# First sums of a graph network: three 14-column tiles for the gathered rows, indices and gathers a block ahead, the overflow added first, the byte stores one block late

## Chip, cores and metric

The kernel runs on one core of one Trainium2 chip. The metric is the device time of one execution in microseconds (us); the time before is the median of three runs. Profiles are of one execution.

## What is computed

The reference is a stack of four graph networks over 6,250 nodes (48 features) and 200,000 edges `src -> dst`. The change touches the first sum of the first network only. Cut to that:

```python
gate = silu(edge_attr @ F1W + F1b) @ F2W + F2b            # per edge
gate = gate + (ei * (ej @ adapt)).sum(-1, keepdims=True)  # ei, ej: embeddings of src and dst
cw   = where(distances < CUT, 0.5 * (cos(pi * distances / CUT) + 1.0), 0.0)
mj   = node_mult[dst]
msg  = gate * h[dst] * (cw * mj)[:, None]
agg  = segment_sum(msg, src, num_segments=N)
tot  = segment_sum(mj, src, num_segments=N)
```

All later layers use the same edges: four layers of attention over `src`, two convolutions, a gated sum, a normalised convolution. So this first pass also leaves in DRAM what they read.

## The kernel before

**Data.** The nodes stand in 49 blocks of 128 (one node per partition). An earlier stage, `build_grid`, has put one 138-number record per edge into DRAM. `grid` has one record per (tail node, head block): for a tail block these are 49 columns of 128 records. A second edge between a tail and the same head block goes to the overflow: `WS[b]` more columns for block `b`, 4 to 28, 502 in all, 10.25 on average.

**The loop.** `first_sums` walks over the 49 tail blocks in the list `ORDER`, whose neighbours have unlike numbers of overflow columns (4, 5, 14, 8, 12, 9, 11, 10, 7, 5, 28, 6 ...). For each block:

- The records come in tiles `recs` of at most 14 columns: four for the grid (14, 14, 14, 7; `load`, L1062, on SP's queue) and one for the overflow, two where it has over 14 columns (L1058).
- `heads_to_rows` copies the head numbers to `hd` (L1128), transposes them on TensorE (L1130), stores them in DRAM as `heads` (L1133) and reads them back, broadcast to all partitions, as `hr` (L1121).
- `hr` against the lane number gives one-hot tiles `hot_b` (L1187, DVE). ACT makes 8-bit copies and stores them for later layers (L1191, L1192).
- TensorE transposes each one-hot square; ACT gathers these in the tile `dt` (L1199, one buffer), a block's 128 rows of the adjacency matrix.
- TensorE picks the head rows of the table by matmuls with the one-hot squares (`pick_rows`, L1007); ACT copies them to `tr` (L1008, two buffers).
- `add` (L1152 to L1178) makes the messages of one piece of up to 14 columns and adds them to `acc`: nine to ten DVE instructions. L1160 adds to the bias, L1177 sums the weights to `ac`, L1165 to L1176 share the single tile `pr`. Two ACT copies with stores keep attributes and gates for later layers (L1155 to L1159).
- `put_rows` (L1231) stores `dt` into `adj` by an indirect DMA from POOL's queue.

**The overflow** can't be picked by one-hots. `overflow` (L1066 to L1108) reads its records, gathers `ei`, the tail's own row (L1073), makes the indices `idx_g` on DVE (L1082) and gathers each column's table rows into `tr_o` with one indirect DMA per column from POOL's queue (L1085). Then it counts how often a cell of `adj` occurs (`same`, `times`, L1090 to L1094) and makes the cell numbers `to` and the 8-bit counts `many` (the tile is named `times_8`, ACT, L1107). `put_cells` writes one byte per partition and column into `adj` (L1112, indirect DMAs on POOL's queue); these must come after the rows of the same block have been written.

**Order.** In the program's text a block does: one-hots; four pieces with their adds, and after the second the load of the next block's grid records; `heads_to_rows` of the next block; the adds of the overflow; the `adj` store; the final sums; `overflow` of the next block; the byte stores of this block. The framework that builds the program places instructions in each engine's queue by priority and by when it believes their operands to be ready, so a queue's order can differ from the text; `keep_in_program_order` (L1162) forbids this for one instruction. Each queue is worked in order. Tiles have a fixed number of buffers (`bufs`, else two in this pool), and an instruction that needs a new one waits for the last reader of the oldest.

Of the kernel before, what the change touches and what calls it, by code (L numbers as in the profile page):

```python
# [18 lines left out]
F32 = mybir.dt.float32  # L19
# [10 lines left out]
N, E, H, R, G, NEL, L = 6250, 200000, 48, 40, 32, 119, 4  # L30
P = 128
# [4 lines left out]
def rows(t, i):  # L36
    return bass.IndirectOffsetOnAxis(ap=t[:, i : i + 1], axis=0)
# [436 lines left out]
NB = 49  # L474
# [55 lines left out]
def chunks(n, k):  # L530
    return [(i, min(k, n - i)) for i in range(0, n, k)]
# [480 lines left out]
def first_sums(ctx: ExitStack, tc: tile.TileContext, g, keep, dram, table0, tails, h, agg, tot):  # L1012
# [39 lines left out]
    def load(b, spans, src):  # L1052

        out = []
        for s0, n in spans:
            t = sp.tile([P, PC, RW], F32, name="recs", bufs=8)
            if src is over:
                nc.sync.dma_start(t[:, :n], over[b, :, s0 : s0 + n])  # L1058
            else:
                for k in range(s0, s0 + n, GD):  # L1060
                    v = g.grid[k * NQ : (k + GD) * NQ].rearrange("(r d) f -> r d f", d=GD)
                    nc.sync.dma_start(t[:, k - s0 : k - s0 + GD], v[b * P : (b + 1) * P])  # L1062
            out.append(t)
        return out

    def overflow(b, hd):  # L1066


        W = WS[b]
        spans = chunks(W, PC)  # L1070
        recs = load(b, spans, over)
        ei = sp.tile([P, 2 * G + H], F32, name="ei")
        nc.gpsimd.indirect_dma_start(out=ei, out_offset=None, in_=tails, in_offset=rows(g.nat, b))  # L1073
        hv = hd[:, NB : NB + W]
        for (s0, n), t in zip(spans, recs):
            nc.vector.tensor_copy(hv[:, s0 : s0 + n], t[:, :n, HD])
        none = sp.tile([P, OS], F32, name="none", bufs=1)
        nc.vector.tensor_scalar(none[:, :W], hv, 0.0, None, OP.is_equal)
        nc.vector.tensor_scalar(g.bias[:, g.col[b] + NB : g.col[b] + NB + W], none[:, :W], -BIG, None, OP.mult)
        ix = g.idx[:, WO[b] : WO[b + 1]]  # L1080
        nc.vector.tensor_scalar(none[:, :W], none[:, :W], float(NQ), -1.0, OP.mult, OP.add)
        nc.vector.tensor_tensor(ix, hv, none[:, :W], OP.add)  # L1082
        tr = sp.tile([P, OS, T0], F32, name="tr_o", bufs=1)
        for w in range(W):
            nc.gpsimd.indirect_dma_start(out=tr[:, w], out_offset=None, in_=table0, in_offset=rows(g.idx, WO[b] + w))  # L1085

        mf = sp.tile([P, OS], F32, name="times", bufs=1)
        for w, n in chunks(W, 12):
            eq = sp.tile([P, 12, NB + OS], BF, name="same", bufs=1)
            nc.vector.tensor_tensor(eq[:, :n, : NB + W], hd[:, None, : NB + W].to_broadcast([P, n, NB + W]),  # L1090
                                    hv[:, w : w + n, None].to_broadcast([P, n, NB + W]), OP.is_equal)
            nc.vector.tensor_tensor(eq[:, :n, NB : NB + W], eq[:, :n, NB : NB + W],
                                    weights[:, w : w + n, :W], OP.mult)
            nc.vector.reduce_sum(mf[:, w : w + n], eq[:, :n, : NB + W], AX.X)  # L1094

        to = sp.tile([P, OS], I32, name="to")
        nc.vector.scalar_tensor_tensor(none[:, :W], mf[:, :W], float(AGAIN), none[:, :W], OP.is_ge, OP.add)
        nc.vector.tensor_scalar(none[:, :W], none[:, :W], -1.0, float(1 << 19), OP.not_equal, OP.mult)
        nc.vector.tensor_tensor(none[:, :W], none[:, :W], nat49[:, b : b + 1].to_broadcast([P, W]), OP.add)
        pl = sp.tile([P, OS], I32, name="pl", bufs=1)  # L1100
        nc.vector.tensor_scalar(pl[:, :W], ix, 7, None, OP.logical_shift_right)
        nc.vector.tensor_tensor(to[:, :W], pl[:, :W], none[:, :W], OP.add)
        nc.vector.tensor_scalar(to[:, :W], to[:, :W], 7, None, OP.logical_shift_left)
        nc.vector.tensor_scalar(pl[:, :W], ix, P - 1, None, OP.bitwise_and)
        nc.vector.tensor_tensor(to[:, :W], to[:, :W], pl[:, :W], OP.bitwise_or)
        many = sp.tile([P, OS // 4], I32, name="times_8")
        nc.scalar.activation(many.bitcast(F8)[:, :W], mf[:, :W], AF.Copy, saturate=False)  # L1107
        return [(NB + s0, n, rec, tr[:, s0 : s0 + n]) for (s0, n), rec in zip(spans, recs)], ei, (to, many)  # L1108

    def put_cells(b, to, many):  # L1110
        for w in range(WS[b]):
# [7 lines left out]
    def heads_of(b, d0, n):  # L1119
        hr = sp.tile([P, PC * P], BF, name="hr")  # L1120
        nc.sync.dma_start(hr[:, : n * P], heads[b : b + 1, d0 * P : (d0 + n) * P].to_broadcast([P, n * P]))  # L1121
        return hr

    def heads_to_rows(b, recs):

        hd = sp.tile([P, NB + OS], F32, name="hd")
        for (s0, n), t in zip(spans, recs):
            nc.vector.tensor_copy(hd[:, s0 : s0 + n], t[:, :n, HD])  # L1128
        pt = tp.tile([NB, P], F32, name="hd_ps")
        nc.tensor.transpose(pt, hd[:, :NB], ident)  # L1130
        ht = sp.tile([NB, P], BF, name="ht")
        nc.vector.tensor_scalar(ht, pt, firsts, None, OP.subtract)
        nc.sync.dma_start(heads[b].rearrange("(d p) -> d p", p=P), ht)  # L1133
        bs = g.bias[:, g.col[b] : g.col[b] + NB]
        nc.vector.tensor_scalar(bs, hd[:, :NB], 1.0, -1.0, OP.min, OP.add)
        nc.vector.tensor_scalar(bs, bs, BIG, None, OP.mult)
        return [heads_of(b, *span) for span in spans[:2]], hd

    recs = load(ORDER[0], spans, g.grid)
    hrs, hd = heads_to_rows(ORDER[0], recs)  # L1140
    others, ei, own_cells = overflow(ORDER[0], hd)
    for pos, b in enumerate(ORDER):
        after = ORDER[pos + 1] if pos + 1 < NB else None
        T = NB + WS[b]
        nc.scalar.copy(h[:, pos], ei[:, 2 * G :])
        lgt = sp.tile([P, NB + OS], F32, name="lgt")
        bs = g.bias[:, g.col[b] : g.col[b] + T]
        ac = sp.tile([P, 8, 1], F32, name="ac")
# [3 lines left out]
        def add(t0, n, rec, tr):  # L1152
            rec = rec[:, :n]
            at = sp.tile([P, PC, R], F32, name="at", bufs=2)
            nc.scalar.copy(at[:, :n], rec[:, :, :R])  # L1155
            nc.scalar.dma_start(g.attr[b, :, t0 : t0 + n], at[:, :n])
            g2 = sp.tile([P, PC, H], F32, name="g2", bufs=2)
            nc.scalar.copy(g2[:, :n], rec[:, :, R + H : CW])
            nc.scalar.dma_start(g.gate[b, :, t0 : t0 + n], g2[:, :n])  # L1159
            i = nc.vector.tensor_add(bs[:, t0 : t0 + n], bs[:, t0 : t0 + n], tr[:, :n, T0 - 1])  # L1160
            if t0 >= NB:
                tc.keep_in_program_order(i)  # L1162

            pr = sp.tile([P, PC, 2 * G], F32, name="pr", bufs=1)
            nc.vector.tensor_mul(pr[:, :n], tr[:, :n, H : H + 2 * G], ei[:, None, : 2 * G].to_broadcast([P, n, 2 * G]))  # L1165
            lg = sp.tile([P, PC, 2], F32, name="lg")
            nc.vector.reduce_sum(lg[:, :n], pr[:, :n].rearrange("p t (k g) -> p t k g", k=2), AX.X)
            nc.vector.tensor_mul(lg[:, :n, 0], lg[:, :n, 0], rec[:, :, CW])
            nc.vector.tensor_mul(lgt[:, t0 : t0 + n], lg[:, :n, 1], rec[:, :, CW])

            ga = pr[:, :, :H]
            nc.vector.tensor_add(ga[:, :n], rec[:, :, R : R + H], lg[:, :n, 0:1].to_broadcast([P, n, H]))
            if not done:
                nc.vector.memset(acc, 0.0)
            nc.vector.tensor_mul(ga[:, :n], ga[:, :n], tr[:, :n, :H])
            nc.vector.tensor_add(acc[:, :n], acc[:, :n], ga[:, :n])  # L1176
            nc.vector.reduce_sum(ac[:, len(done)], tr[:, :n, T0 - 2], AX.X)  # L1177
            done.append(t0)  # L1178


        dt = sp.tile([P, NB, P], F8, name="dt", bufs=1)
# [11 lines left out]
        for i, (s0, n) in enumerate(spans):  # L1193
# [8 lines left out]
            add(s0, n, recs[i], tr)  # L1202
            if i == 1 and after is not None:
                ahead = load(after, spans, g.grid)
        if after is not None:
            hrs, hd = heads_to_rows(after, ahead)
        for piece in others:
            add(*piece)
        i = put_rows(tc, g.adj, g.nat, b, dt.rearrange("p d q -> p (d q)").bitcast(I32), "adj")
        tc.declare_no_dep(i.ins, group="cells", reason="the cells before are in rows of other nodes")  # L1210
        cells_of = b, *own_cells
        nc.scalar.dma_start(g.logit[b, :, :T], lgt[:, :T])
        add_up(nc, acc, PC, agg[:, pos])
        nc.vector.reduce_sum(tot[:, pos : pos + 1], ac[:, : len(done)].rearrange("p i o -> p o i"), AX.X)
        if after is not None:
            recs = ahead
            others, ei, own_cells = overflow(after, hd)
        put_cells(*cells_of)


def add_up(nc, t, n, to):
# [622 lines left out]
```

## Time and profile before

| | us |
|---|---|
| median of 3 runs (lowest, highest) | 12119.19 (12105.58, 12132.64) |
| the profiled execution, its own time | 12122.53 |
| its span, first to last instruction | 12120.7 |
| 3760 to 6160 of the span, which holds the first sums | 2400.00 |
| of these: DVE busy | 1429.62 |
| POOL busy | 1193.94 |
| ACT busy | 1153.64 |
| PE busy | 819.84 |

The share of the 16 DMA engines in that part is 0.68 on average, at 221 GB/s. Busy times are sums over instructions of one engine; register work and the issue of DMAs by SP and ACT are not in them. An indirect DMA's row on POOL is the making of its descriptors; when its data lands is seen only from who waits for it. In the views, "<- X" names what released an instruction that had been waiting.

### The profile page before, as it was taken

Reading aid. Unit: us, or ns where it says so; the run is one execution under the profiler, and the core shown is the slowest. Engines: PE = TensorE matmul, PEld = TensorE weight load, DVE = VectorE, ACT = ScalarE, POOL = GpSimd, SP = SyncE. Lnnn points to the kernel's source line nnn. Section 1 sums busy time; section 2 is a strip of 40 time slices with the busy share of each in tenths; the row PEclk is TensorE's granted clock in tenths of the full one; section 3 lists DMA queues with packets and bytes.
Section 4 is the critical chain, followed back from the end, with each engine's and each line's share of the span. In section 5 each row is a group of like instructions: output and inputs, shape, how many; then the busy total and the mean of one; then the engine's idle time right before and its main releaser. Section 6 shows DMA issues by size and latency. Waiting matters only on the chain. (4 is left out here: it accounts for less than half of the span.)

```text
span 12120.7 us, 180061 instructions
## 1 busy us (share of the span) xinstructions
PE 5280.4 (44%) x67611; PEld 4656.0 (38%) x67611; DVE 7874.7 (65%) x16470; ACT 3855.5 (32%) x9495; POOL 7176.8 (59%) x5713
## 2 busy tenths in 40 slices
PE   1166555555452333333334444443444444582226
PEld 1144443344342333333234443443444344482226
DVE  7756555555554655566569888887988888515443
ACT  0044434334333544544433223222322222111111
POOL 0257555555554455545548886886888688408880
PEclk9986666666666666666656666666766667796558
DMA  8845222222225766667634434443443444555445
GB/s 292 288 142 171 71 64 67 67 64 67 67 66 165 238 211 220 225 218 231 202 115 129 129 119 119 127 126 105 137 125 119 124 124 130 164 167 145 130 125 153
DMA packets 970521, 1742.53 MB, mean 144 GB/s; under 512 B 478058, under 2 KB 686158, under 8 KB 911909
## 3 DMA queue, kind: packets, MB, share of 16 engines
q1 hardware_dynamic: 645378, 1038.72, 27.2%
q0 software_dynamic: 188320, 315.39, 10.9%
q10 hardware_dynamic: 135936, 376.80, 8.0%
q8 instruction: 531, 8.70, 0.3%
q14 instruction: 356, 2.92, 0.1%
HBM read 1176.43 MB, written 561.07 MB: 143 GB/s over the span
## 5 line engine op out<-in xcount | busy, mean ns | idle before, releaser
L1258 POOL DMA_INDIRECT over<-table_k,idx_g x2008 | 3019.2, 1504 | 670.7 <-issue 570.2
L1007 PEld LDWEIGHTS <-hot_t 128*128 128x128 fp8e4 x36015 | 1870.1, 112 | 2475.7 <-issue 2446.7
L975 POOL DMA_INDIRECT grid<-rec,sloti x1666 | 1744.2, 1047 | 1333.3 <-DVE rec L946 704.0
L1007 PE MATMUL pick_ps<-k_parts,hot_t 128*128 128x96 bf16 x28812 | 1643.2, 231 | 1715.0 <-ACT kh L1008 1532.1
L1008 ACT COPY kh<-pick_ps 128x480 f32<-128x480 f32 (+1 forms) x1960 | 982.8, 568 | 1395.1 <-DVE sm L1227 566.2
L1258 POOL DMA_INDIRECT over<-table_g,idx_g x502 | 714.3, 1423 | 593.2 <-DMA lg<-logit 440.5
L971 PE MATMUL pg<-w,hid 97*128 97x96 f32 x3332 | 655.2, 348 | 811.1 <-ACT hid L968 803.8
L971 PEld LDWEIGHTS pg<-w,hid 97*128 97x128 f32 x3332 | 568.3, 249 | 892.9 <-ACT hid L968 872.6
L1112 POOL DMA_INDIRECT adj<-times,to x502 | 576.5, 1148 | 453.1 <-DMA adj<-dt,nat 252.1
L916 ACT ACTIVATE junk<-dup_ps,less 128x128 bf16<-128x128 f32 x1666 | 590.2, 365 | 435.3 <-PE dup_ps L913 388.1
L1007 PE MATMUL pick_ps<-table_b,hot_b 128*128 128x114 bf16 x7203 | 596.5, 266 | 257.8 <-ACT tr L1008 257.8
L901 DVE TENSOR_TENSOR pick<-look_ps,sb 128x441 f32<-128x441 f32 x588 | 347.3, 591 | 548.3 <-PE look_ps L899 536.6
L1007 PEld LDWEIGHTS <-hot_b 128*128 128x128 bf16 x7203 | 575.9, 130 | 264.6 <-issue 264.4
L972 DVE TENSOR_TENSOR rec<-pg,cut 128x384 f32<-128x384 f32 (+1 forms) x441 | 235.2, 534 | 625.9 <-PE pg L971 625.3
L1225 DVE TENSOR_TENSOR kh<-kh 128x1152 f32<-128x1152 f32 (+4 forms) x980 | 609.9, 623 | 0.0
L1085 POOL DMA_INDIRECT tr_o<-table,idx_g x502 | 493.1, 982 | 174.6 <-issue 144.8
L1007 PE MATMUL pick_ps<-g_parts,hot_t 128*128 128x48 bf16 x7203 | 261.4, 203 | 711.9 <-ACT xe L1008 634.9
L1198 PE MATMUL dt_ps<-f_identb,hot_b 128*128 128x128 bf16 x2401 | 244.3, 270 | 701.4 <-DVE hot_b L1187 550.3
L1421 PE MATMUL h_ps<-x_parts,am 128*128 128x144 bf16 (+1 forms) x7203 | 475.6, 228 | 125.7 <-DMA am<-adj 76.6
L1421 PEld LDWEIGHTS <-am 128*128 128x128 fp8e4 x7203 | 470.0, 99 | 126.7 <-ACT x_f L1409 74.9
L1326 DVE TENSOR_TENSOR kh<-kh,sc 128x2352 f32<-128x2352 f32 x196 | 509.8, 2601 | 9.3 <-ACT sc L1323 9.1
L1316 DVE TENSOR_TENSOR kh<-kh,agg 128x2352 f32<-128x2352 f32 x196 | 509.5, 2600 | 0.1
(419 smaller groups left out, 13577.9 us busy)
## 6 DMA issues: line engine op xcount, KB each, us to landing
hot_t<-hot SPq DMA_DIRECT2D x245, 784.0 KB
grid<-zero ACTq DMA_DIRECT2D x150, 1127.0 KB
recs<-grid SPq DMA_DIRECT2D x348, 483.0 KB
am<-adj SPq DMA_DIRECT2D x147, 784.0 KB
hr<-heads_g SPq DMA_DIRECT2D x147, 448.0 KB
low<-lows SPq DMA_DIRECT2D x49, 1088.0 KB
gate_g<-g ACTq DMA_DIRECT2D x156, 336.0 KB
attr_g<-at ACTq DMA_DIRECT2D x156, 280.0 KB
```

Source lines behind the costliest of these rows:

```text
L916: nc.scalar.activation(junk, ps[:, t], AF.Sign, bias=less13[:, way : way + 1], accum_out=dup[:, t0 + t : t0 + t + 1])
L971: nc.tensor.matmul(pg[:, k], ht[:, k * P : (k + 1) * P], w2, start=True, stop=True)
L975: i = nc.gpsimd.indirect_dma_start(out=g.grid, out_offset=rows(sloti, t), in_=rec[:, t, :], in_offset=None, bounds_check=SLOTS - 1, oob_is ...
L1007: nc.tensor.matmul(ps[:, d], hot(db0 + d0 + d), parts[:, db0 + d0 + d, k], start=(k == 0), stop=(k == 2))
L1008: nc.scalar.copy(dst[:, d0 : d0 + m], ps[:, :m])
L1085: nc.gpsimd.indirect_dma_start(out=tr[:, w], out_offset=None, in_=table0, in_offset=rows(g.idx, WO[b] + w))
L1112: i = nc.gpsimd.indirect_dma_start(out=cells, out_offset=rows(to, w), in_=many.bitcast(U8)[:, w : w + 1], in_offset=None, bounds_check=NQ ...
L1225: nc.vector.tensor_add(t[:, :k], t[:, :k], t[:, n - k : n])
L1258: self.tc.nc.gpsimd.indirect_dma_start(out=t[:, w], out_offset=None, in_=self.table, in_offset=rows(self.g.idx, WO[b] + w0 + w))
L1316: nc.vector.tensor_mul(k, k, q[:, pos : pos + 1].to_broadcast([P, n, H]))
L1326: nc.vector.tensor_mul(v, v, sc[:, :NB, None].to_broadcast([P, NB, H]))
L1421: nc.tensor.matmul(to, a8[:, b, d * P : (d + 1) * P], parts[:, b0 + b].rearrange("p k f -> p (k f)"), start=(b0 + b == 0 and d % CB == 0), ...
```

## The change

- `tr_o` was one tile of 28 columns; it becomes one tile of 14 columns per overflow piece, from three buffers. `recs` goes from eight buffers to seven.
- `overflow` is cut in two. Its first half (head numbers, indices, `ei`, gathers) now runs for the next block at the top of this one; its second half, `cells_to` (counts and cell numbers), stays at the end of the block.
- The overflow records are loaded one block earlier (`load_over(pos + 2)` at the end of a block).
- The overflow pieces are added first in a block, ahead of the one-hots, and are no longer held in program order.
- A block's byte stores are issued in the next block, after its second piece, and those of the last block after the loop.

```diff
--- before.py
+++ after.py
@@ -1053,7 +1053,7 @@
 
         out = []
         for s0, n in spans:
-            t = sp.tile([P, PC, RW], F32, name="recs", bufs=8)
+            t = sp.tile([P, PC, RW], F32, name="recs", bufs=7)
             if src is over:
                 nc.sync.dma_start(t[:, :n], over[b, :, s0 : s0 + n])
             else:
@@ -1063,12 +1063,11 @@
             out.append(t)
         return out
 
-    def overflow(b, hd):
-
+    def overflow(b, recs):
 
         W = WS[b]
         spans = chunks(W, PC)
-        recs = load(b, spans, over)
+        hd = sp.tile([P, NB + OS], F32, name="hd")
         ei = sp.tile([P, 2 * G + H], F32, name="ei")
         nc.gpsimd.indirect_dma_start(out=ei, out_offset=None, in_=tails, in_offset=rows(g.nat, b))
         hv = hd[:, NB : NB + W]
@@ -1080,9 +1079,20 @@
         ix = g.idx[:, WO[b] : WO[b + 1]]
         nc.vector.tensor_scalar(none[:, :W], none[:, :W], float(NQ), -1.0, OP.mult, OP.add)
         nc.vector.tensor_tensor(ix, hv, none[:, :W], OP.add)
-        tr = sp.tile([P, OS, T0], F32, name="tr_o", bufs=1)
-        for w in range(W):
-            nc.gpsimd.indirect_dma_start(out=tr[:, w], out_offset=None, in_=table0, in_offset=rows(g.idx, WO[b] + w))
+        out = []
+        for (s0, n), rec in zip(spans, recs):
+            tr = sp.tile([P, PC, T0], F32, name="tr_o", bufs=3)
+            for w in range(n):
+                nc.gpsimd.indirect_dma_start(out=tr[:, w], out_offset=None, in_=table0,
+                                             in_offset=rows(g.idx, WO[b] + s0 + w))
+            out.append((NB + s0, n, rec, tr))
+        return out, ei, (hd, none)
+
+    def cells_to(b, hd, none):
+
+        W = WS[b]
+        hv = hd[:, NB : NB + W]
+        ix = g.idx[:, WO[b] : WO[b + 1]]
 
         mf = sp.tile([P, OS], F32, name="times", bufs=1)
         for w, n in chunks(W, 12):
@@ -1105,7 +1115,7 @@
         nc.vector.tensor_tensor(to[:, :W], to[:, :W], pl[:, :W], OP.bitwise_or)
         many = sp.tile([P, OS // 4], I32, name="times_8")
         nc.scalar.activation(many.bitcast(F8)[:, :W], mf[:, :W], AF.Copy, saturate=False)
-        return [(NB + s0, n, rec, tr[:, s0 : s0 + n]) for (s0, n), rec in zip(spans, recs)], ei, (to, many)
+        return to, many
 
     def put_cells(b, to, many):
         for w in range(WS[b]):
@@ -1121,9 +1131,8 @@
         nc.sync.dma_start(hr[:, : n * P], heads[b : b + 1, d0 * P : (d0 + n) * P].to_broadcast([P, n * P]))
         return hr
 
-    def heads_to_rows(b, recs):
-
-        hd = sp.tile([P, NB + OS], F32, name="hd")
+    def heads_to_rows(b, recs, hd):
+
         for (s0, n), t in zip(spans, recs):
             nc.vector.tensor_copy(hd[:, s0 : s0 + n], t[:, :n, HD])
         pt = tp.tile([NB, P], F32, name="hd_ps")
@@ -1134,15 +1143,23 @@
         bs = g.bias[:, g.col[b] : g.col[b] + NB]
         nc.vector.tensor_scalar(bs, hd[:, :NB], 1.0, -1.0, OP.min, OP.add)
         nc.vector.tensor_scalar(bs, bs, BIG, None, OP.mult)
-        return [heads_of(b, *span) for span in spans[:2]], hd
+        return [heads_of(b, *span) for span in spans[:2]]
+
+    def load_over(pos):
+        b = ORDER[pos]
+        return load(b, chunks(WS[b], PC), over)
 
     recs = load(ORDER[0], spans, g.grid)
-    hrs, hd = heads_to_rows(ORDER[0], recs)
-    others, ei, own_cells = overflow(ORDER[0], hd)
+    others, ei, found = overflow(ORDER[0], load_over(0))
+    hrs = heads_to_rows(ORDER[0], recs, found[0])
+    own_cells = cells_to(ORDER[0], *found)
+    next_over = load_over(1)
+    cells_before = None
     for pos, b in enumerate(ORDER):
         after = ORDER[pos + 1] if pos + 1 < NB else None
         T = NB + WS[b]
         nc.scalar.copy(h[:, pos], ei[:, 2 * G :])
+        er = ei
         lgt = sp.tile([P, NB + OS], F32, name="lgt")
         bs = g.bias[:, g.col[b] : g.col[b] + T]
         ac = sp.tile([P, 8, 1], F32, name="ac")
@@ -1158,11 +1175,9 @@
             nc.scalar.copy(g2[:, :n], rec[:, :, R + H : CW])
             nc.scalar.dma_start(g.gate[b, :, t0 : t0 + n], g2[:, :n])
             i = nc.vector.tensor_add(bs[:, t0 : t0 + n], bs[:, t0 : t0 + n], tr[:, :n, T0 - 1])
-            if t0 >= NB:
-                tc.keep_in_program_order(i)
 
             pr = sp.tile([P, PC, 2 * G], F32, name="pr", bufs=1)
-            nc.vector.tensor_mul(pr[:, :n], tr[:, :n, H : H + 2 * G], ei[:, None, : 2 * G].to_broadcast([P, n, 2 * G]))
+            nc.vector.tensor_mul(pr[:, :n], tr[:, :n, H : H + 2 * G], er[:, None, : 2 * G].to_broadcast([P, n, 2 * G]))
             lg = sp.tile([P, PC, 2], F32, name="lg")
             nc.vector.reduce_sum(lg[:, :n], pr[:, :n].rearrange("p t (k g) -> p t k g", k=2), AX.X)
             nc.vector.tensor_mul(lg[:, :n, 0], lg[:, :n, 0], rec[:, :, CW])
@@ -1176,6 +1191,12 @@
             nc.vector.tensor_add(acc[:, :n], acc[:, :n], ga[:, :n])
             nc.vector.reduce_sum(ac[:, len(done)], tr[:, :n, T0 - 2], AX.X)
             done.append(t0)
+
+        if after is not None:
+            others_next, ei, found = overflow(after, next_over)
+        for piece in others:
+            add(*piece)
+        others = others_next
 
 
         dt = sp.tile([P, NB, P], F8, name="dt", bufs=1)
@@ -1202,20 +1223,22 @@
             add(s0, n, recs[i], tr)
             if i == 1 and after is not None:
                 ahead = load(after, spans, g.grid)
+            if i == 1 and cells_before is not None:
+                put_cells(*cells_before)
         if after is not None:
-            hrs, hd = heads_to_rows(after, ahead)
-        for piece in others:
-            add(*piece)
+            hrs = heads_to_rows(after, ahead, found[0])
         i = put_rows(tc, g.adj, g.nat, b, dt.rearrange("p d q -> p (d q)").bitcast(I32), "adj")
         tc.declare_no_dep(i.ins, group="cells", reason="the cells before are in rows of other nodes")
-        cells_of = b, *own_cells
+        cells_before = b, *own_cells
         nc.scalar.dma_start(g.logit[b, :, :T], lgt[:, :T])
         add_up(nc, acc, PC, agg[:, pos])
         nc.vector.reduce_sum(tot[:, pos : pos + 1], ac[:, : len(done)].rearrange("p i o -> p o i"), AX.X)
         if after is not None:
             recs = ahead
-            others, ei, own_cells = overflow(after, hd)
-        put_cells(*cells_of)
+            own_cells = cells_to(after, *found)
+        if pos + 2 < NB:
+            next_over = load_over(pos + 2)
+    put_cells(*cells_before)
 
 
 def add_up(nc, t, n, to):
```

## Prediction

> **What bounds the kernel now.** The change touches one stage only, so I first cut the span there. In the timeline the rows of L1231 (one store of `adj` per block) run from 3810.43 to 6141.08 us: 48 steps in 2330.7 us, 48.6 us a block. The windows view of that stretch (time, then busy us of PE, PEld, DVE, ACT, POOL, then clock, DMA share, GB/s):
>
> ```profile
> 3810.40:6141.20 2330.80, 800.50 (x9456) 759.61 (x9456) 1400.30 (x3841) 1126.02 (x1777) 1180.85 (x1090) 0.63 0.67 221
> ```
>
> No engine is busy for more than 60% (DVE, 29.2 us a block), so the stage is a chain of waits. The waits view of the stretch names them (who waited, for whom, us in total, times, longest):
>
> ```profile
> DVE ac L1177 <- DMA tr_o<-table,idx_g: 623.7, 48, 21.9
> ...
> POOL adj L1231 <- ACT dt L1199: 535.3, 43, 31.6
> ...
> POOL adj L1112 <- DMA adj<-dt,nat: 242.9, 37, 10.4
> ```
>
> DVE, the busiest engine, stands still once a block until the gathers of the overflow rows have landed. POOL, which issues them, waits for ACT's last copy of `dt`, then for the landing of the `adj` store. The groups view gives POOL's prices (busy, mean ns, idle before):
>
> ```profile
> L1112 POOL DMA_INDIRECT adj<-times,to x496 | 570.5, 1150 | 442.5 <-DMA adj<-dt,nat 242.9 <-issue 141.5 <-DVE lg L1167 22.5
> L1085 POOL DMA_INDIRECT tr_o<-table,idx_g x498 | 489.3, 982 | 161.7 <-issue 143.9 <-DVE pr L1175 8.2 <-DMA tr_o<-table,idx_g 3.7
> ```
>
> With 0.29 us of issue between two, a byte store takes 1.44 us and a gather 1.27; a block has 10.25 of each on average (502 columns in 49 blocks): 14.8 and 13.0 us. The timeline shows the ring over one block:
>
> ```profile
> 4828.55 1.62 POOL L1231 DMA_INDIRECT adj<-dt,nat  x1 [11.09 <-ACT dt L1199]
> ...
> 4836.96 0.15 DVE L1082 TENSOR_TENSOR idx_g<-hd,none 128x8 int32<-128x8 f32 x1
> ...
> 4838.89 1.04 POOL L1112 DMA_INDIRECT adj<-times,to  x1 [8.72 <-DMA adj<-dt,nat]
> ...
> 4863.32 0.95 POOL L1085 DMA_INDIRECT tr_o<-table,idx_g  x1 [0.31 <-issue]
> ...
> 4867.34 0.17 DVE L1177 TENSOR_REDUCE ac<-tr_o 128x1 f32<-128x8 f32 x1 [14.46 <-DMA tr_o<-table,idx_g]
> ...
> 4876.77 1.62 POOL L1231 DMA_INDIRECT adj<-dt,nat  x1 [12.50 <-ACT dt L1199]
> ```
>
> `adj` store, 10.3 us to its landing, 11 byte stores, 8 gathers, 3 us to land, DVE goes on, 9.4 us to the next `adj` store: 48.2 us, all in series. The index of the gathers is there at 4837.1, 16 us before POOL begins them. Note also that L1177 of the overflow stands first in DVE's queue, although the text adds the overflow last: queues are ordered by the framework, by when it believes operands are ready.
>
> DMA bounds it next: in the window 4833 to 4849 the share is 0.98 at 358 GB/s, in 4849 to 4869 it is 0.45. The stage moves 514.3 MB, 10.7 MB a block, or 29.9 us at 358 GB/s.
>
> **The change, part by part.** Durations are of the profiled execution (12122.5 us; span 12120.7), 3.3 us above the median of the runs, 12119.2.
>
> *The stall.* Gathers for the next block are issued at the top of this one and used at the top of the next, so DVE no longer meets them in flight. L1177 gives 623.7 us, the same wait at L1160 another 41.4: 665.1 us, 13.9 a block. Between zero and all of it goes; I take all, since a gather that starts at the index (4837.1) lands after 1.35 (`ei`) + 13.0 + 2.6 = 17 us, well inside a block. What is late next is ACT's copy of the first picked columns: in the block of 4802 DVE waited 2.05 us for it. The overflow add, now at the top, has some 4 us of DVE work without it and fills that. Left: 48.6 - 13.9 = 34.7 us a block.
>
> *Byte stores a block late.* Count and price stay, but they no longer wait for the landing (242.9 us of POOL) and stand after piece 1, ahead of this block's `adj` store on POOL. POOL's sum is 1.35 + 13.0 + 14.8 + 1.8 = 31 us, below 34.7. From the index at 4837.1, gathers and byte stores end at 4864.9; `dt` would be ready at 4828.3 + 34.7 = 4863.0, so the `adj` store goes 2 us late. What hides that: `dt` has one buffer and its next copy came at 4845.53, 17 us after the last, while the landing takes 10.3: 6.7 us to spare. Cost 0; where columns of two blocks exceed about 24 (11 of 47 pairs) lateness reaches ACT one for one, within the next term.
>
> *The wait that comes in.* `to` and `times_8` have two buffers, and each now lives a block longer. L1102 (DVE) and L1107 (ACT) of block b+2 wait until the byte stores of block b, behind the gathers of b+2, have landed. Queued behind L1107 are ACT's `at`, `g2`, `hot_8`, `dt` and `tr` copies; behind L1102 all of DVE, with the next index (`none` has one buffer). So a block can't be shorter than 1.35 + 1.27 W(b+2) + 1.44 W(b) + 2.6 + 1.5 (rest of the cell numbers and the new index). Over the order of blocks (4, 5, 14, 8, 12 ... columns) this is 33.9 on average; summed where it exceeds 34.7, 122 us, or 2.6 a block. If the index also comes 4.5 us later it is 4.9 a block; if buffers never collide, 0. I take 2.6, from the rows' own prices: 125 us.
>
> *DMA.* Same bytes in less time: at 39 us the queues move 275 GB/s, 77% of the full window. DVE's waits for `recs` and `hr` are 96.9 + 41.3 + 78.5 = 216.7 us, 4.5 a block. They may stay (0) or double (4.5); I take half, 2.2, or 108 us. In this trace SP waited 2.8 us on average, at most 6.1, for the 12 KB `heads` store.
>
> The Trainium skill's page "DMA: Bandwidth & Descriptors", section "Latency and other measured facts", gives an HBM access as 0.2 us on average and 2 us at high load, which speaks against closing the gaps. By an estimate from it, `recs`, `heads` and `hr` in series would each take 1.8 us more, 259 us in all, and the sum would end near 11,840; no row here isolates such an access.
>
> *Seven `recs` buffers, overflow loaded a block ahead.* The fourth grid tile waits for piece 1 instead of piece 0, 5.4 us later (one 14-column add). Its chain (load 3.5, `heads` 1.4, `hr` 1.5 + 5.8) ended 4.9 us before L1187 used it, and the overflow add may run ahead of L1187: 0, at worst 5.4 a block (259 us). The load on SP (0.32 us) stays behind the first two `hr` loads.
>
> *Moved at no cost.* Index arithmetic (6 DVE instructions of 0.17 us), `ei` and the gathers keep their number. Splitting `tr_o` into tiles of 14 adds none.
>
> Sum: 12122.5 - 665 + 125 + 108 = 11,690 us: 39.6 us a block, 3.5% faster.
>
> **The rivals.**
>
> *The stall survives in part.* L1177 of the next overflow can be put into this block's queue, before its gathers land. For: it stood early before, and the order kept on L1160 is gone. Against: it stood 16 us after the index in DVE's queue, and the landing now comes 17 us after it. Were it 8 us earlier, a stall of 9 us would remain: 13.9 - 9 = 4.9 us a block gained, 11,885.
>
> *Slower: the gathers slide behind this block's `adj` store.* If the index of b+1 comes late (`none` has one buffer), POOL has `adj` first: 1.8 + 1.35 + 13.0 + 2.6 after `dt`, then the overflow add (at most 5.4), now ahead of L1187 on DVE, then 22.8 us from L1187 to the last `dt` (4839.5 to 4876.8, less the stall): 47.0, with DMA's 2.2 49.2. It turns slower past 48.6; 0.64 x 48 = 31 us, 12,150, and each byte store that stands between adds 1.44. Against: in the timeline above the index stands 40 us ahead of the next `adj` store.
>
> *Nothing changes.* The queues come out in the old order: 12,120.
>
> **How the numbers follow.** Forecast 11,690, chance 0.66; stall in part (11,885) 0.19; slower (12,150) 0.12; nothing 0.03. All terms at their best give 12122 - 665 = 11,457; stall gone and the three costs at their worst together (235 + 217 + 259) 12,170. The range 11,480 to 11,980 leaves out slower, nothing and little at the ends. About 0.2%, 24 us, is what the runs can tell from no change (they spread over 27 us). Faster 0.85, same 0.03, slower 0.12.
>
> **What would show it.** Right: between the first and last L1231 about 1,900 us instead of 2331; DVE's wait for `tr_o` below 100 us; the byte stores' wait for the landing of `adj` near 0; DMA share near 0.8; new waits of L1102 or L1107 on `adj<-times,to`. Wrong: `tr_o` still at the head of DVE's waits (stall in part), or gathers after L1231 in POOL's timeline with DVE idle before L1187 (slower). If DMA's share stands near 1, the DMA term was too small.

## The result, and the profile after

| | us, median (lowest, highest), 4 runs each |
|---|---|
| before, beside these runs | 12115.53 (12105.58, 12132.64) |
| after | 12190.55 (12176.05, 12195.98) |
| ratio, 95% interval | 1.0055 (1.0043 to 1.0067) |

The change makes the kernel 0.55% slower. The forecast was 11,690, and the time lies outside its range, on the other side of before. The profiled execution of after has a span of 12174.2 us. In it the rows of L1254 (the `adj` store, L1231 before) run from 3802.70 to 6211.10 us: 48 steps of 50.2 us instead of 48.6. That is 77.7 us more in this stage, against 75.0 us in the medians.

The windows view of this stretch of after (time, then busy us of PE, PEld, DVE, ACT, POOL, then clock, DMA share, GB/s):

```profile
3802.70:6211.10 2408.40, 777.09 (x9456) 734.77 (x9456) 1394.77 (x3830) 1133.33 (x1787) 1187.32 (x1085) 0.62 0.68 215
```

Every engine does the work of before within 4%. What has changed is only waiting. The waits view of DVE in the stretch (who, for whom, us in total, times, longest):

```profile
DVE bias L1177 <- DMA tr_o<-table,idx_g: 592.9, 50, 23.8
DVE hot_b L1208 <- DMA hr<-heads_g: 136.2, 74, 6.1
DVE hd L1137 <- DMA recs<-grid: 110.3, 96, 3.9
DVE bias L1177 <- ACT tr L1008: 69.5, 20, 4.8
DVE hd L1075 <- DMA recs<-grid: 45.0, 37, 3.6
DVE bias L1177 <- DMA adj<-times,to: 41.2, 2, 24.0
```

The stall that the change was to remove is still there: 592.9 us, and 634.1 with the last row, in which L1177 waits at the same place (665.1 before). It stands at the bias sum now, L1177 (L1160 before), not at the weight sum, L1192 (L1177 before). Three other waits have grown: for `hr` from 78.5 to 136.2 us, for the picked columns `tr` from 19.4 to 69.5, for `recs` from 138.2 to 155.3. Together: -31.0 + 57.7 + 50.1 + 17.1 = +93.9 us, less 5.5 us of DVE work: +88, against the 77.7 that the stage lost; a few small waits of before, 14.9 us in all, are gone too (0.4 left).

The waits view of POOL and of ACT in the same stretch:

```profile
POOL adj L1254 <- ACT dt L1220: 608.6, 47, 24.0
POOL adj L1122 <- DMA adj<-dt,nat: 253.5, 48, 8.0
...
ACT h_rows L1161 <- DMA ei<-tails,nat: 498.8, 46, 16.1
```

The byte stores (L1122) still wait for the landing of an `adj` store, 253.5 us against 242.9: in POOL's queue they still follow the `adj` store of their own block. ACT has a wait of its own for `ei`, whose gather is queued with those of the table rows.

The timeline shows why, over one block (rows of POOL and DVE; start, us, engine, line; in brackets the idle time before it and what ended it):

```profile
4817.64 1.23 POOL L1254 DMA_INDIRECT adj<-dt,nat  x1 [11.33 <-ACT dt L1220]
4824.33 2.55 POOL L1122 DMA_INDIRECT adj<-times,to  x1 [5.46 <-DMA adj<-dt,nat]
...
4833.43 0.15 DVE L1081 TENSOR_TENSOR idx_g<-hd,none 128x8 int32<-128x8 f32 x1
...
4836.19 0.99 POOL L1072 DMA_INDIRECT ei<-tails,nat  x1 [0.30 <-issue]
...
4838.91 0.16 DVE L1111 TENSOR_SCALAR pl<-idx_g 128x8 int32<-128x8 int32 x1
...
4842.63 0.99 POOL L1086 DMA_INDIRECT tr_o<-table,idx_g  x1 [0.31 <-issue]
...
4851.51 0.95 POOL L1086 DMA_INDIRECT tr_o<-table,idx_g  x1 [0.30 <-issue]
...
4855.25 0.17 DVE L1177 TENSOR_TENSOR bias<-bias,tr_o 128x8 f32<-128x8 f32 x1 [16.18 <-DMA tr_o<-table,idx_g]
...
4855.41 1.04 DVE L1208 TENSOR_SCALAR hot_b<-hr,lane 128x1792 bf16<-128x1792 bf16 x2
...
4860.77 0.18 DVE L1177 TENSOR_TENSOR bias<-bias,tr 128x14 f32<-128x14 f32 x1 [4.23 <-ACT tr L1008]
```

On POOL the kinds come in the order of before: `adj` store, its landing, the byte stores of the same block, gathers, the next `adj` store. Only the gathers are for a block further on. The index of these gathers (8 columns, L1081) is there at 4833.6, but the gathers begin at 4842.6 and end at 4852.5. On DVE the bias sum that waits has 8 columns too: it is the overflow of the **next** block, in the queue of this one, and stands there 5.5 us after its index (the work before it ends at 4839.1). In the block of before that the prediction shows, the same stall (14.46 us) sat behind all of the block's `hot_b` instructions, ahead of its first piece. Now it sits ahead of the second half of `hot_b` as well; the one-hots come 16 us late, TensorE's picks after them, and DVE waits another 4.23 us for `tr`. So the gathers were issued a block ahead as the text says, and their first reader was pulled a block ahead with them. The rows of the whole stage say the same (waits for `tr_o` of over 1 us, 52 in before and 50 in after): from the index to the landing it was 30.1 us on average and is 21.7, DVE's work and other waits in between took 17.4 us and take 9.9, so the stall went only from 12.8 to 11.9.

### The profile page after: what moved, and what is told of

It reads as the page before. It is cut to its first block, busy times and chain, and to the rows that moved or that the text cites. A ratio compares the mean times of both kernels' runs of the same rounds, so it can differ in the third digit from the quotient of the medians.

```text
span 12174.2 us, 180036 instructions
## 1 busy us (share of the span) xinstructions
PE 5249.2 (43%) x67611; PEld 4623.9 (38%) x67611; DVE 7870.0 (65%) x16470; ACT 3856.5 (32%) x9495; POOL 7160.0 (59%) x5713
## 5 line engine op out<-in xcount | busy, mean ns | idle before, releaser
L1122 POOL DMA_INDIRECT adj<-times,to x502 | 595.4, 1186 | 401.4 <-DMA adj<-dt,nat 253.5
L1007 PE MATMUL pick_ps<-table_b,hot_b 128*128 128x114 bf16 x7203 | 563.0, 258 | 348.1 <-ACT tr L1008 347.4
L1007 PEld LDWEIGHTS <-hot_b 128*128 128x128 bf16 x7203 | 544.3, 124 | 359.5 <-issue 359.3
L1219 PEld LDWEIGHTS <-hot_b 128*128 128x128 bf16 x2401 | 213.1, 128 | 955.1 <-DVE hot_b L1208 656.2
```

The costliest lines, as they stand in the source:

```text
L1007: nc.tensor.matmul(ps[:, d], hot(db0 + d0 + d), parts[:, db0 + d0 + d, k], start=(k == 0), stop=(k == 2))
L1122: i = nc.gpsimd.indirect_dma_start(out=cells, out_offset=rows(to, w), in_=many.bitcast(U8)[:, w : w + 1], in_offset=None, bounds_check=NQ ...
L1219: nc.tensor.transpose(pd[:, k], hot[d // HC][:, d % HC * P : (d % HC + 1) * P], identb)
```

## The experiments

Each changes one kernel by a few lines. Times are medians; ratios are to runs of before on the same chip, and runs of different groups are compared by their ratios. A group is e1 to e4 (before 12119.65), e5 to e8 (12114.87) and e9 to e12 (12108.93). "Pinned" means that an instruction keeps its place in the text on its engine.

**e1: after, with the two sums of the overflow pinned on DVE.**

```diff
             i = nc.vector.tensor_add(bs[:, t0 : t0 + n], bs[:, t0 : t0 + n], tr[:, :n, T0 - 1])
+            if t0 >= NB:
+                tc.keep_in_program_order(i)
...
-            nc.vector.reduce_sum(ac[:, len(done)], tr[:, :n, T0 - 2], AX.X)
+            i = nc.vector.reduce_sum(ac[:, len(done)], tr[:, :n, T0 - 2], AX.X)
+            if t0 >= NB:
+                tc.keep_in_program_order(i)
```

> The changed kernel with the overflow piece's two early-ready DVE sums (bias, L1177, and weight sum, L1192) held in program order behind what was traced before them on DVE. Queue theory (the stall survived because both sums of the next block stand in DVE's queue a few us behind the index, ahead of byte stores and gathers): DVE's wait for tr_o falls from 593 us to under 100, and the time to about 11,850, since ACT's stand for ei (499 us) is left. ACT theory (the stand of ACT at L1161 sets the pace): DVE's idle time only moves to tr or hot_b, 12,150 to 12,190. Buffer theory (seven recs buffers and full DMA set the pace): the idle time moves to hr and recs, about 12,150.

Measured 12040.48 us, ratio 0.9938 (0.9921 to 0.9955). That lies between the queue theory's 11,850 and the ACT theory's 12,150. The wait for `tr_o` is gone from DVE, but others have grown, these two most. The waits view of e1 in the stage (46.8 us a block):

```profile
DVE bias L1177 <- ACT tr L1008: 418.9, 47, 12.8
...
ACT h_rows L1161 <- DMA ei<-tails,nat: 565.6, 45, 17.1
```

The place of the two sums is worth 1.2% against after (0.9938 against 1.0055). The rest of the stall has moved to ACT: L1161 copies the next block's row `ei`, whose gather (L1072) is in the same ring on POOL, and ACT's copies of `dt` and `tr` are queued behind it.

**e2: after, with that copy on ACT pinned alone.**

```diff
-        nc.scalar.copy(h[:, pos], ei[:, 2 * G :])
+        tc.keep_in_program_order(nc.scalar.copy(h[:, pos], ei[:, 2 * G :]))
```

> The changed kernel with ACT's copy of the tail rows (L1161) held in program order, so that it no longer stands in ACT's queue in front of the copies of the block before. Queue theory: ACT's wait for ei goes, but DVE still stands for tr_o, so 12,120 to 12,190. ACT theory: about 11,800, and DVE's wait for tr_o shrinks with it. Buffer theory: 12,150.

Measured 12178.85 us, ratio 1.0049 (1.0032 to 1.0065): as after. ACT no longer waits for `ei`, DVE still waits 555.3 us for `tr_o`. In after's block above, ACT's wait for `ei` ends at 4842.2 and DVE's for `tr_o` at 4855.3: the wait that ends first is worth nothing when it is taken out alone.

**e3: both, e1 and e2 together.**

> The changed kernel with all three held in program order (two DVE sums and ACT's copy). Queue and ACT theory together: the block falls from 50 us to about 39, as in the prediction's sum, 11,690 (11,600 to 11,850). Buffer theory: no more than 1% below the kernel before, 12,000 or more.

Measured 11864.16 us, ratio 0.9784 (0.9767 to 0.9800). The two pins together take off 2.7% of before's time, where they took 1.2% and 0.1% alone. The timeline shows the repair: the sum behind the index of 8 columns is now that of the block before, with 11 columns, long landed.

```profile
4715.39 0.16 DVE L1081 TENSOR_TENSOR idx_g<-hd,none 128x8 int32<-128x8 f32 x1
4715.46 0.17 DVE L1177 TENSOR_TENSOR bias<-bias,tr_o 128x11 f32<-128x11 f32 x1
```

Windows and waits of e3 in the stage, 43.1 us a block:

```profile
3816.40:5886.10 2069.70, 739.21 (x9456) 702.38 (x9456) 1401.19 (x3829) 1132.84 (x1788) 1227.51 (x1084) 0.64 0.77 250
```

```profile
DVE hd L1137 <- DMA recs<-grid: 207.9, 129, 4.8
DVE bias L1177 <- ACT tr L1008: 194.2, 47, 7.1
DVE hot_b L1212 <- DMA hr<-heads_g: 164.7, 105, 4.2
DVE hd L1075 <- DMA recs<-grid: 72.3, 40, 4.1
DVE to L1112 <- DMA adj<-times,to: 8.0, 2, 6.4
...
POOL adj L1122 <- DMA adj<-dt,nat: 324.5, 48, 13.6
```

DVE's waits account for the gain: the 665.1 us for `tr_o` are gone; the waits for `recs`, `hr` and `tr` rose by 142.0, 86.2 and 174.8 us. -665.1 + 403.0 = -262.1, and the stage is 2330.7 - 2069.7 = 261.0 us shorter.

**e4: before, with its weight sum alone pinned (L1177 of before), and nothing of the change.**

> The kernel before with one instruction held in program order, the weight sum of the overflow piece (L1177), and nothing else of the change. Queue theory: the 624 us in front of it go, and with the pinned bias sum late in the block the gathers land in time: 11,600 to 11,750 without any gather a block ahead. Rival (the gathers are too late for their own block whatever the order, and must be made a block ahead): the wait moves to L1160 or L1165 and at most half is gained, about 11,900 to 12,100.

Measured 11858.44 us, ratio 0.9782 (0.9765 to 0.9798), between the two expectations. The wait for `tr_o` fell from 665.1 to 233.8 us; it stands at the bias sum, as the rival said, but more than half of the stall is gained. From the waits view of e4 in the stage:

```profile
DVE bias L1160 <- DMA tr_o<-table,idx_g: 233.8, 27, 32.9
DVE hd L1128 <- DMA recs<-grid: 182.2, 127, 4.7
DVE hot_b L1189 <- DMA hr<-heads_g: 69.0, 65, 6.7
...
DVE hd L1076 <- DMA recs<-grid: 27.4, 20, 3.5
```

One order on one instruction brings as much as the whole change with three (e3). So the change's own moves, taken together and with one `recs` buffer fewer, add nothing to what the order of the queues gives. What they are worth with eight buffers wasn't tried.

**e5: e3, and the byte stores queued on POOL behind the last gather that was issued before them.**

```diff
-                nc.gpsimd.indirect_dma_start(out=tr[:, w], out_offset=None, in_=table0,
+                gathered[0] = nc.gpsimd.indirect_dma_start(out=tr[:, w], out_offset=None, in_=table0,
...
-            i = nc.gpsimd.indirect_dma_start(out=cells, ...
+            with tc.issue_after(gathered[0].ins):
+                i = nc.gpsimd.indirect_dma_start(out=cells, ...
```

> The change, with the three pins of e3, and the byte stores queued behind the last gather that was issued before them on POOL. Queue theory: POOL's ring is what is left in e3 (43.1 us a block = some 25.6 busy, 6.5 between issues, 6.8 waiting for the landing of adj, 4.2 waiting for dt); with gathers instead of byte stores behind the adj store, the 324.5 us of waiting for its landing fall below 60 and the stage ends at 36 to 38 us a block: 11,550 to 11,650 us. Buffer theory: the wait of to and times_8 for byte stores now comes in, up to 125 us: 11,700, with L1112 or L1117 waiting for adj<-times,to. DMA theory: at 43 us a block the queues already move 250 GB/s; the landing is late because they are full, so the landing wait only changes its place and the time stays at 11,820 to 11,870.

Measured 11894.86 us, ratio 0.9821 (0.9805 to 0.9837), 0.4% above e3: no expectation but the last comes near. Of its mechanism the waits show one half, a wait that changes its place; that full queues are the reason they don't show.

```profile
POOL tr_o L1086 <- DVE lgt L1188: 183.7, 32, 8.8
POOL ei L1072 <- DVE pr L1184: 168.2, 25, 11.6
...
POOL tr_o L1086 <- DVE idx_g L1081: 81.3, 10, 12.7
```

The wait for the landing fell to 5.4 us. In its place POOL stands in front of gathers that DVE has yet to release (their index or a buffer), with byte stores behind them that could go: each order puts one of two waits, landing or index, in POOL's way. DVE's own wait of `to` for the byte stores (L1112, the buffer theory's) rose from 8.0 to 58.1 us; the stage is 34.9 us longer than e3's.

**e6: before, with the byte stores behind the gathers and no pin.**

> The kernel before, with the byte stores queued behind the last gather on POOL and nothing else. Queue theory: the gathers begin at their index instead of 26 us later, and land before the weight sum L1177 stands at the head of DVE's queue (some 14 to 16 us after the index), so the wait for tr_o falls from 665 us to 50 to 150 and the landing wait of 242.9 us goes: 11,550 to 11,700 us, although the weight sum stands as early as before. If the weight sum's place is the cause by itself, the wait for tr_o stays above 400 us and the time above 11,950. DMA theory: 11,820 to 11,870.

Measured 11972.82 us, ratio 0.9886 (0.9869 to 0.9902). The queue theory was too low by 270 us; time and wait are nearly those of the other branch (above 11,950, above 400 us), in which the weight sum's early place is the cause by itself. The weight sum (L1179 here) still waits, with 24 of the waits put down to the byte stores' landings:

```profile
DVE ac L1179 <- DMA adj<-times,to: 221.1, 24, 12.8
DVE ac L1179 <- DMA tr_o<-table,idx_g: 168.0, 22, 12.7
```

That is 389.1 us, 8.1 a block, instead of 665.1. The gathers didn't begin at their index: the one buffer of `tr_o` is read by the overflow before until 4807.2 in the block whose index is ready at 4795.0, and the first gather goes at 4807.46. A better order on POOL takes less than half of the stall; the sum's early place keeps the rest.

**e7: e4 and e6 together.**

> The kernel before, with the weight sum pinned as in e4 and the byte stores behind the gathers as in e6. Queue theory: within 0.7% of e6 and of e5 (11,520 to 11,680), since either edit alone takes most of the stall and POOL's 31 us, DVE's 29 us and the data's 30 us are next. DMA theory: no faster than e4, 11,840 to 11,870.

Measured 11848.18 us, ratio 0.9775 (0.9758 to 0.9791): no different from e4. The wait for `tr_o` fell from 233.8 to 33.2 us; in its place comes the wait that the forecast had priced at 125 us:

```profile
DVE to L1102 <- DMA adj<-times,to: 174.0, 28, 24.1
...
ACT times L1107 <- DMA adj<-times,to: 354.3, 29, 25.8
```

**e8: after, with only the line given back that the change took away (the bias sum pinned).**

> The change, with the one line given back that it took away: the overflow's bias sum keeps its place in the text on DVE. Queue theory: the weight sum (L1194) still has no pin and stands in front of this block's first sums, behind the same gathers; DVE's wait for tr_o moves to it and stays above 400 us, 12,130 to 12,200 us. Rival, that the lost line alone is the cause: the wait goes and the time is that of e1, 12,020 to 12,060.

Measured 12195.02 us, ratio 1.0063 (1.0046 to 1.0080). The wait goes to the next reader:

```profile
DVE ac L1194 <- DMA tr_o<-table,idx_g: 547.8, 45, 20.4
```

So the removed line is not the cause by itself. Either of the two sums may stand early, and one is enough for the whole loss.

**e9: e3, with the byte stores two blocks late and four buffers of `to` and `times_8`.**

```diff
-            if i == 1 and cells_before is not None:
-                put_cells(*cells_before)
+            if i == 1 and len(waiting) > 1:
+                put_cells(*waiting.pop(0))
...
-        cells_before = b, *own_cells
+        waiting.append((b, *own_cells))
```

> The change with the three pins of e3, and the byte stores two blocks late instead of one (to and times_8 with four buffers): the byte stores that stand behind an adj store on POOL are then those of the block before, whose own adj store landed some 40 us ago. Ring theory: the wait for the landing (324.5 us in e3, 6.8 a block) goes below 30 us and the stage ends at 38 to 40 us a block, 11,650 to 11,750. Data theory: e3 stands on DVE, which does 29 us of work a block and waits 13.3 us more for records, heads and the picked columns behind them (207.9 + 72.3 + 164.7 + 194.2 us); POOL's wait is slack, and the time stays at 11,840 to 11,890 although the wait for the landing goes.

Measured 11844.90 us, ratio 0.9787 (0.9770 to 0.9804), the same as e3. It doesn't tell the two theories apart, since the wait didn't go: 302.7 us. Byte stores of an older block still wait for the last `adj` store ahead of them; that their dependence covers `adj` as a whole would explain it and wasn't tested.

**e10: e4 with seven `recs` buffers instead of eight.** (`bufs=8` to `bufs=7`.)

> The kernel before with the weight sum pinned as in e4, and seven recs buffers instead of eight, as the change has. The forecast put this at 0, at worst 259 us. Buffer theory: SP already waits 1,000 us and more for a recs buffer, so a buffer less delays the loads by the time of a piece: 11,900 to 12,100, with DVE's waits for recs above the 209.6 us of e4. If 0 was right: 11,840 to 11,880.

Measured 11943.09 us, ratio 0.9862 (0.9846 to 0.9879): 0.0080 above e4, 97 us. DVE's waits for `recs` rose from 209.6 to 267.7 us, those for `hr` from 69.0 to 111.6 and for `tr` from 66.3 to 334.8 (the wait for `tr_o`, 233.8 in e4, is 0.8 here). ACT stands at `h_rows` for `ei`, 286.5 us. With the buffer count the framework also lays out the queues anew (the orders on DVE and ACT differ from e4's), so the 97 us are those of both.

**e11: e10 with four more loads of 483 KB a block, which nothing reads.**

```diff
+            more = sp.tile([P, GD, RW], F32, name="more", bufs=1)
+            v = g.grid[i * GD * NQ : (i + 1) * GD * NQ].rearrange("(r d) f -> r d f", d=GD)
+            nc.scalar.dma_start(more, v[b * P : (b + 1) * P])
```

> e10 with four more loads of 483 KB a block on ACT's queue into a tile of their own that nothing reads: 1.93 MB on top of 10.7, 5.4 us a block at 358 GB/s, 259 us in all. Data theory (the records and heads arrive late because the queues are full of other data): 80 to 260 us above e10, nearly all of it in DVE's waits for recs and hr. If those waits are latencies in series, and the queues have room (share 0.78): below 40 us above e10, and a share near 0.9.

Measured 12015.89 us, ratio 0.9928 (0.9906 to 0.9949): 72.8 us above e10, for data that take 259 at full rate. The waits view of DVE and of ACT, and the end of the windows line of e11 (share 0.84, 272 GB/s) show queues with room, records that come later, and ACT, which issues the added loads, standing for their landings:

```profile
DVE hd L1128 <- DMA recs<-grid: 401.4, 145, 9.4
DVE bias L1160 <- ACT tr L1008: 144.1, 55, 4.9
DVE hot_b L1189 <- DMA hr<-heads_g: 126.4, 84, 5.3
DVE hd L1076 <- DMA recs<-grid: 92.8, 46, 8.0
```

```profile
ACT at L1155 <- DMA more<-grid: 115.2, 36, 9.5
...
ACT dt L1201 <- DMA more<-grid: 110.1, 45, 4.7
```

```profile
3808.30:6048.20 2239.90, 763.29 (x9456) 712.47 (x9456) 1431.51 (x3850) 1116.11 (x1780) 1198.16 (x1089) 0.64 0.84 272
```

The waits for `recs` rose by 226.5 us and that for `tr` fell by 190.7. But the added loads share one buffer, and ACT's 225.3 us of waits for them, and a new order of DVE's and ACT's queues (ACT's 286.5 us for `ei` are gone), came in with the data. The result lies just below the data theory's bound and above the other's, and the 72.8 us can't be put down to the data alone.

**e12: e7 with three buffers of `to` and `times_8`,** the fastest version.

```diff
-        to = sp.tile([P, OS], I32, name="to")
+        to = sp.tile([P, OS], I32, name="to", bufs=3)
...
-        many = sp.tile([P, OS // 4], I32, name="times_8")
+        many = sp.tile([P, OS // 4], I32, name="times_8", bufs=3)
```

> e7 with three buffers of to and times_8 instead of two. Buffer theory: the waits of e7 for adj<-times,to (174.0 us at L1102 on DVE, 354.3 at L1107 on ACT) go below 60 together, and the time falls by 80 to 200 us: 11,650 to 11,770. Data theory: they go, and the waits for recs, hr and tr take their place: 11,820 to 11,860.

Measured 11770.05 us, ratio 0.9716 (0.9700 to 0.9732): 0.0059 below e7, 71 us, just under the buffer theory's 80 to 200. The wait of `times` on ACT fell from 354.3 to 33.1 us, that of `to` left the list, and the single buffer of `dt` came next:

```profile
ACT dt L1203 <- DMA adj<-dt,nat: 175.2, 20, 23.4
```

Of the change it has only later byte stores, in another form; it is 3.4% faster than after.

## Why the prediction was wrong

**The step that failed: "The stall."** It read the text's order as the queue's: "used at the top of the next, so DVE no longer meets them in flight". The forecast's own reading of before held the warning, that L1177 stood first in DVE's queue though the text adds the overflow last. The runs showed in its place that the sums went ahead with the gathers: 634.1 of the 665.1 us stayed. What decides most of the stall is how soon behind the index the sums that read these gathers stand on DVE; gathers a block ahead in the text took only 31.0 us off it in after. e1 and e8 show it from one side (both sums pinned, no wait for `tr_o`; one pinned, 547.8 us at the other), e4 from the other (one pin in before brings the wait from 665.1 to 233.8 us, and 2.2% of the time, without the change). The rest of it does hang on when the gathers run: in e7, with e4's pin, gathers ahead of the byte stores bring 233.8 us down to 33.2.

**The rival "The stall survives in part" named the place, and was sized wrong.** Its sentence, that L1177 of the next overflow can be put into this block's queue before its gathers land, is what the timeline shows. Against it the forecast set "it stood 16 us after the index"; were the sum 8 us nearer, with the landing 17 us after the index, 9 us would be left. The sum did come nearer by about as much (17.4 to 9.9 us on average, 5.5 in the block above, where half of `hot_b` and part of the overflow's own piece no longer stand in between). The landing is what was mis-sized: 21.7 us after the index, on average and in this block (4833.6 to 4855.3), not 17. Byte stores still go ahead of the gathers, six of them here (7.7 us). So 16.2 us remain in this block and 11.9 on average, not 9; and 11,885 has no term for the waits that grew. The sign that the forecast gave for this rival, `tr_o` still at the head of DVE's waits, came.

**"They no longer wait for the landing" failed** for the same reason on POOL: issued after the second piece in the text, the byte stores were ready first in the queue and stayed there (253.5 us). The slower rival expected gathers behind this block's `adj` store; in after they are ahead of it (4842.6 against 4869.1). Its 12,150 is only 41 us off, but by luck, since its mechanism isn't there. After came slower by another way: nearly the same stall, part of it ahead of `hot_b`, and new waits behind it. For `tr` the block above shows it (4.23 us). For `hr` (+57.7 us) it is not shown: one `recs` buffer fewer raised that wait by 42.6 us in e10 too, and the two weren't separated. "Nothing changes", at 0.03, has the order on POOL right, but for which block the gathers are, and its time is nearer than the forecast's, 70 us off.

**The terms, with the stall truly gone (e3, 43.1 us a block against 39.6 forecast).** The stall's 665 us is right there. The data term was 108 us, and the waits that it was to cover rose by 142.0 + 86.2 = 228. It need not all be the price of more data in less time. In e4, with eight buffers and 249 GB/s against 250, the two waits rose by only 61.9 us together (beside 233.8 us of waiting for `tr_o`, which can hide some lateness); from e4 to e10, with seven buffers, they rose by another 100.7. So a part of the 228 may belong to the buffer that the forecast put at 0. The orders of the queues differ as well, so how much stays open. The estimate from the Trainium skill's "DMA: Bandwidth & Descriptors", "Latency and other measured facts", was 259 us for records, heads and `hr`. The 228 is near it in size, but no run shows that it is HBM access time.

The forecast's "What is late next is ACT's copy of the first picked columns", which the overflow add "fills", was put at 0 and cost 174.8 us: the pinned add is done before the last one-hots (at 4719.6 in the block shown for e3, whose picks end the wait at 4731.0), so DVE has nothing left when the picks are awaited. The wait of `to` was 125 us and measured 8: it was to come from byte stores behind the gathers, and in e3 they still follow the `adj` store of their own block. Where they did stand behind the gathers it came, in blocks as long: in e7 (42.8 us) with 174.0 us on DVE and 354.3 on ACT, worth 71 us when removed. 11,690 - 125 + 8 + 120 + 175 = 11,868; e3 measured 11,864. Two slips in that working change nothing in the sum: the bound on a block averages 33.8 us by its own prices, not 33.9, and 4864.9 leaves out the 1.35 us of `ei`, so the `adj` store would go 3 us late rather than 2.

**Seven `recs` buffers** were put at 0, at worst 259. In e10 they cost 97 us with the queues as they then fell. How much of that is in after wasn't tried.

**Prices.** A byte store's mean busy time was 1.15 us in the groups view of before and is 1.19 in after; a gather's is 0.98 and 0.99. These held, as did DVE's work.

Still open: what part of the 43 us is the chain of records, heads, `hr`, one-hots and picks, and what part POOL's ring. Versions that change POOL's order (e5, e7, e9) end within 0.5% of each other, and none changes the chain alone.

## What to carry to other kernels

Before pricing an earlier load, find in the timeline who reads it first on each in-order queue, and for which block: if the queue's builder moved that reader ahead before, it will follow the load, and the wait comes with it. Look on every engine (here it was two DVE sums and one ACT copy): removing one moves the wait to the next, and together they gained more (2.7%) than one by one (1.2 and 0.1%). When a chain of waits is taken out, add up what its neighbours then wait: here 403 of 665 us came back.

## What the hardware showed unexpectedly

- An `adj` store of 128 rows of 6,272 bytes (803 KB) landed 5.46 us after its descriptors were made in the block above, and 8.72 us in before's. The Trainium skill's "DMA: Bandwidth & Descriptors", "Anatomy of one DMA — SWDGE (gpsimd) path", fits 2.0 us + bytes / 436e3; an estimate from it is 3.8 us. These two are longer; over the stage of before, POOL's waits for this landing run from 3.4 to 10.4 us.
- POOL's price for the same indirect DMAs differs between versions: a byte store took 1150 ns on average in before and 1241 in e5, a gather 982 and 1094; POOL's busy time in the stage was 1180.9 against 1267.6 us. It isn't simply that they run denser: in e9, whose blocks are as short, a gather took 1118 but a byte store 1140. Most single rows are 0.95 to 1.0 us, with some of 1.5 us and more among them. The cause wasn't tested.
